# Zero products and the guard ahead of spreads, changed in the scans of the second layer

## The chip, the cores and the metric

The kernel runs as one program on one core of a Trainium2 chip. The metric is the device time of one execution in microseconds, and the figure compared is the median over runs. The engines are called TensorE (PE in the profile, PEld for its weight loads), VectorE (DVE), ScalarE (ACT), GpSimd (POOL) and SyncE (SP, which here only issues DMA transfers).

## The reference, cut to what matters

The network has four layers over 4 images of 64x64 positions and 96 channels. The first two layers are state space layers. Each expands to 192 inner channels, orders the 4096 positions of an image in four ways, and runs a recurrence with 16 states for each channel along each order:

```python
def step(h, inp):
    dt, u, Bl, Cl = inp
    h = h * jnp.exp(dt[..., None] * A) + (dt * u)[..., None] * Bl[:, :, None, :]
    y = jnp.einsum('bkdn,bkn->bkd', h, Cl)
    return (h, y)
```

For one image of one layer that is 4 orders x 192 channels x 16 states x 4096 steps. The two layers compute this in the same way and differ in the orders (diagonals and rings in the first layer; rows and columns, forwards and backwards, in the second), and in what is made of the sums afterwards. A feed-forward part of the second layer and the layers three and four follow; they have nothing to do with the change.

## The kernel before

**Tiling of a scan.** One *batch* is one image of one layer; there are eight, the first four of the first layer. A batch has 16 *segments* (four orders x four stretches of 1024 steps). A segment has 6 *channel blocks* of 32 channels, and a block has 4 *groups* of 4 states, so that a group is a tile of 128 partitions (32 channels x 4 states) by 1024 steps. A segment thus has 24 groups and a batch 384.

**What a group does** (lines of the kernel before):

- `spread_u` (L1098), once for a block: TensorE multiplies `dt*u` of 32 channels by a matrix of ones and zeros, which copies every channel to 4 partitions. Two products of 512 columns, each of them two rows in the profile, fill the PSUM tile `u`. There is one such tile, so the spread of the next block waits until the last group of this block has read it.
- `decay` (L1105): ScalarE computes `da`, the exponential of `dt*A`. Four buffers.
- `enter` (L1109): VectorE multiplies `u` by the B factors and writes `t`.
- `recur` (L1116): VectorE runs the recurrence over 1024 steps and writes `h`.
- `leave` (L1131): GpSimd multiplies `h` by the C factors and writes `hc`.
- `collect` (L1141): TensorE adds the 4 states of every channel into the PSUM tile `y`, four products of 256 columns side by side in the array (8 rows in the profile). `y` holds two blocks, so a pair of blocks is open at a time.

VectorE's order is fixed by hand: two enters, then two recurrences, and so on. Seen from the spread of a block: it becomes ready when the last enter of the block before has ended; VectorE then still has the last two recurrences of that block to do; after these it needs the new `u`.

After the last collect of a pair ScalarE copies `y` out (`copy_y`, L1177), TensorE transposes the copy (`turn`, L1189, 4 products) into the PSUM bank `m`, and ScalarE copies the result into rows (`keep_rows`, L1195).

**The next segment** is prepared beside this one (`prepare`). TensorE turns the inputs (`turn_x`, L923), multiplies them by the projections (L963) and adds four terms of the softplus in PSUM (`add`, L1047, 16 products for a segment, here called *sums of the softplus*). Each result goes through the same single bank `m`, and ScalarE must take it out (L937, L976, L978, L1050) before the next product can write there. ScalarE also does the pointwise steps (L1013 to L1021) and the logarithm (L1039).

**The order of the work** is computed while the program is built. `batch` hands all operations of a batch to a `Flow` with a cost, a due time and what each depends on. `Flow.run` takes the operation that can start first, by its own clock; among those that start within 0.1 us it takes the one that is due first. The spreads, decays, enters, recurrences and leaves are *hard*: while a hard operation of an engine is still to come, another operation of that engine is taken only if it is due earlier, or ends some time ahead of the hard one's due time. That time, the *guard*, is 4.2 us for TensorE and 0.5 us for the others. Each engine then executes its own list strictly in order, each instruction waiting for its semaphores.

Whenever an operation of TensorE is placed, `Flow` calls `keep_busy` (L1151) with the gap that the plan has ahead of it, less 2.0 us if the operation is hard (a spread) and less 0.1 us if not. `keep_busy` fills that gap with *zero products* (L1166): 32 columns of zeros times 256 columns, one for every 0.43 us. They leave the sums as they are. They are written into the open half of `y` (adding zero), or, when the last collected group was the last of its block, into the half that the next block will begin anew, or into the next `y` tile once the old one has been copied.

Between batches `side_by_side` runs the merging of one image and the projections and convolutions of another; the change does not touch it.

Of the kernel before, what the change touches and what calls it, by code (L numbers as in the profile page):

```python
# [38 lines left out]
NSG = NS // GS  # L39
# [3 lines left out]
class Kit:  # L43


    def __init__(self, tc, pool):
        self.tc, self.nc = tc, tc.nc
        nc = self.nc
        self.ident = self.t(pool, [128, 128], "ident")
        make_identity(nc, self.ident)  # L50
        self.eps = self.t(pool, [128, 1], "eps")
        nc.vector.memset(self.eps, 1e-5)
# [71 lines left out]
class Flow:  # L124

    def __init__(self, fill):
        self.fill, self.ops = fill, []

    def add(self, *args, **kw):
        op = Op(*args, **kw)
# [3 lines left out]
    def run(self):  # L136
        inside = set(map(id, self.ops))
        for op in self.ops:
            op.deps = [d for d in op.deps if id(d) in inside]
            op.left = len(op.deps)  # L140
            for d in op.deps:
                d.users.append(op)
        for op in reversed(self.ops):
            for d in op.deps:
                due = op.due - d.occ - (0.0 if d.engine == op.engine else d.lat)
                d.due = due if d.due is None else min(d.due, due)
        free, ready, hard = {}, {}, {}
        for op in self.ops:
            free.setdefault(op.engine, 0.0)
            ready.setdefault(op.engine, [])  # L150
            if op.hard:
                hard.setdefault(op.engine, []).append(op)
        for ops in hard.values():
            ops.sort(key=lambda op: -op.due)
        for op in self.ops:
            if not op.left:
                ready[op.engine].append(op)
        bank, drift, left, strict = 0.0, 0.0, len(self.ops), True
        while left:
            best = None  # L160
            for engine, ops in ready.items():
                if not ops:
                    continue
                first = hard.get(engine, [])
                while first and first[-1].left < 0:
                    first.pop()
                when = lambda op: max(free[engine], op.seen, op.after, bank if op.bank > 0 else 0.0)
                fits = ops
                if strict and first:
                    limit = first[-1].due + drift - (4.2 if engine == "PE" else 0.5)  # L170
                    fits = [
                        op
                        for op in ops
                        if op.hard or op.due <= first[-1].due or when(op) + op.occ <= max(limit, free[engine])
                    ]
                    if not fits:
                        continue
                soonest = min(map(when, fits))
                if soonest == math.inf:
                    continue  # L180
                op = min((op for op in fits if when(op) <= soonest + 0.1), key=lambda op: op.due)
                if best is None or when(op) < best[0]:
                    best = when(op), op
            if best is None:
                assert strict
                strict = False
                continue
            strict = True
            start, op = best
            engine = op.engine  # L190
            if engine == "PE":
                self.fill(free[engine], start - free[engine] - (2.0 if op.hard else 0.1))
            op.emit()
            left -= 1
            op.left = -1
            ready[engine].remove(op)
            done = op.fin = start + op.occ
            free[engine] = done
            if op.bank:
                bank = math.inf if op.bank > 0 else done + op.lat  # L200
            if engine == "DVE":
                drift = max(0.0, start - op.due)
            for user in op.users:
                near = user.engine == engine and not op.lands
                user.seen = max(user.seen, done if near else done + op.lat + op.slack)
                user.left -= 1
                if not user.left:
                    ready[user.engine].append(user)
        return drift
# [170 lines left out]
class Stream:  # L380
# [467 lines left out]
    def fetch(self, seg):  # L848
# [31 lines left out]
        if seg.bt.lay.ordered and seg.kd < 2:  # L880

            for j in range(SEG // 128):
                at = seg.i * SEG + j * 128
                seg.turned[j] = []
                for pos, n, token, step in diagonal_runs(seg.kd, at, at + 128):
                    ops.append(Op("SP", 0.1, partial(run, j, pos - at, n, token, step), lat=4.0))
                    seg.turned[j].append((pos - at, n, step < 0))
        elif seg.bt.lay.ordered:
            ops += [Op("POOL", 1.25, partial(gather, j), lat=4.0) for j in range(SEG // 128)]
        elif seg.kd % 2 == 0:  # L890
            ops.append(Op("SP", 0.1, whole, lat=5.0))
        else:
            ops += [Op("SP", 0.1, partial(columns, w), lat=5.0) for w in range(2)]
# [254 lines left out]
            )  # L1148
        self.open = None if gr.sg == NSG - 1 and cb % 2 else gr

    def keep_busy(self, now, gap):  # L1151


        lay = self.layers[0]
        if self.open:
            start = self.open.sg == NSG - 1
            half = 1 if start else self.open.cb % 2
            y = self.open.seg.y[:GC, half * 256 : (half + 1) * 256]
        elif self.vacant and now > self.vacant.fin + 0.5:
            if self.next_y is None:  # L1160
                self.next_y = self.k.t(self.ps_y, [128, CH], "y")
            y, start = self.next_y[:GC, :256], True
        else:
            return
        for _ in range(int(gap / 0.43)):
            self.nc.tensor.matmul(  # L1166
                y,
                self.zeros,
                lay.diag.rearrange("p h t c -> p (h t c)")[:, :256],
                start=start,  # L1170
                stop=start,
                tile_position=(0, 0),
            )
# [57 lines left out]
    def batch(self, segs):  # L1231


        slot, length = 6.74, 6.74 * NCB * NSG / 2
        flow, last = Flow(self.keep_busy), segs[-1]
        add = flow.add
        groups = {}
        dve = []
# [8 lines left out]
        for n, seg in enumerate(segs):  # L1247
            base, o, nxt = n * length, seg.o, seg.next
            prev = segs[n - 1] if n else None
            if nxt:  # L1250
# [5 lines left out]
                if far:  # L1256
                    far.fetched = self.fetch(far)
                    free = [nxt.o["X", j] for j in range(0, SEG // 128, 2)]
# [3 lines left out]
            for i in range(NG):  # L1262
# [6 lines left out]
                if sg == 0:  # L1269
                    if (n, cb) != (0, 0):  # L1270
# [14 lines left out]
                        hard=True,  # L1285
# [7 lines left out]
                    hard=True,  # L1293
# [8 lines left out]
                    hard=True,  # L1302
# [4 lines left out]
                for g2 in (groups[n, i - 1], gr):  # L1307
                    k0 = n * NG + g2.g
                    of = lambda name, back: groups[divmod(k0 - back, NG)].__dict__.get(name) if k0 >= back else None
                    start = base + i // 2 * slot + 2.24 + g2.g % 2 * 2.25  # L1310
# [7 lines left out]
                        hard=True,  # L1318
# [3 lines left out]
                    if not ends:  # L1322
# [8 lines left out]
                        hard=True,  # L1331
# [1107 lines left out]
```

## Time and profile before

| | us |
|---|---|
| median of 3 runs | 15246.63 (15242.52 to 15286.9) |
| profiled execution, its own time | 15391.0 |
| its span, first to last instruction | 15389.1 |
| VectorE busy in the span | 12831.6 (83%) |
| TensorE busy in the span | 13751.2 (89%) |
| VectorE idle ahead of `t` (enter), whole span | 281.2, of it 207.5 released by `u` on PE |
| mean granted TensorE clock | 0.88 of full speed |

The page gives, for each group of instructions, its line, engine, operation, operands and count, then the busy time, the mean duration of one in ns, and the idle time of its engine just before it with what ended that idle time. A product in 32-bit floats takes two rows of TensorE. Granted clock is the share of full speed at which TensorE ran; 0.50 in a stretch means half speed throughout.

### The profile page before, as it was taken

Reading aid. Unit: us, or ns where it says so; the run is one execution under the profiler, and the core shown is the slowest. Engines: PE = TensorE matmul, PEld = TensorE weight load, DVE = VectorE, ACT = ScalarE, POOL = GpSimd, SP = SyncE. Lnnn points to the kernel's source line nnn. Section 1 sums busy time; section 2 is a strip of 40 time slices with the busy share of each in tenths; the row PEclk is TensorE's granted clock in tenths of the full one; section 3 lists DMA queues with packets and bytes.
Section 4 is the critical chain, followed back from the end, with each engine's and each line's share of the span. In section 5 each row is a group of like instructions: output and inputs, shape, how many; then the busy total and the mean of one; then the engine's idle time right before and its main releaser. Section 6 shows DMA issues by size and latency. Waiting matters only on the chain. (4 is left out here: it accounts for less than half of the span.)

```text
span 15389.1 us, 225440 instructions
## 1 busy us (share of the span) xinstructions
PE 13751.2 (89%) x88567; PEld 5562.3 (36%) x88567; DVE 12831.6 (83%) x9645; ACT 8289.2 (54%) x13549; POOL 9204.4 (60%) x4657
## 2 busy tenths in 40 slices
PE   7999899989998999899989998999899889998877
PEld 3333333333333333333333333333333344443344
DVE  1999799969996999699979997999899856565655
ACT  3666466646664666466646665666566423232333
POOL 0898589858985888577747774777577620000123
PEclk9889888878898889888889898888899899998888
DMA  2333433343334333433343334333433400000122
GB/s 79 111 126 125 140 112 126 122 140 112 126 126 139 117 119 127 138 121 114 127 140 123 124 120 146 126 124 111 155 119 119 143 10 11 19 18 13 52 70 71
DMA packets 679264, 1639.33 MB, mean 107 GB/s; under 512 B 102822, under 2 KB 301227, under 8 KB 674428
## 3 DMA queue, kind: packets, MB, share of 16 engines
q1 hardware_dynamic: 641340, 1549.37, 31.7%
q0 software_dynamic: 36864, 75.55, 1.7%
q8 instruction: 700, 11.47, 0.3%
q14 instruction: 360, 2.95, 0.1%
HBM read 1295.03 MB, written 329.58 MB: 106 GB/s over the span
## 5 line engine op out<-in xcount | busy, mean ns | idle before, releaser
L1131 POOL TENSOR_TENSOR hc<-h,bc 128x1024 f32<-128x1024 f32 x3072 | 7203.9, 2363 | 2404.4 <-DVE h L1116 1934.0
L1116 DVE TENSOR_TENSOR_SCAN h<-da,state,t 128x1024 f32<-128x1024 f32 x2304 | 5276.6, 2333 | 30.6 <-ACT state L1127 18.5
L1105 ACT ACTIVATE da<-dts,L_A_logs 128x1024 f32<-128x1024 f32 x3072 | 3510.2, 1149 | 1237.7 <-DVE h L1116 1195.6
L1109 DVE TENSOR_TENSOR t<-u,bc 128x1024 f32<-128x1024 f32 x3072 | 3598.2, 1218 | 281.2 <-PE u L1098 207.5
L1166 PE MATMUL y<-L_diag,zeros 96*32 96x256 f32 x9734 | 2635.8, 410 | 0.0
L1141 PE MATMUL y<-hc,gather_y 128*32 128x256 f32 x24576 | 2434.5, 440 | 35.6 <-POOL hc L1131 34.8
L1098 PE MATMUL u<-dtu,spread 32*128 32x512 f32 x3072 | 1756.5, 696 | 523.9 <-DVE t L1109 517.2
L1116 DVE TENSOR_TENSOR_SCAN h<-da,t 128x1024 f32<-128x1024 f32 x768 | 1711.3, 2270 | 13.0 <-ACT da L1105 8.8
L1166 PEld LDWEIGHTS y<-L_diag,zeros 96*32 96x32 f32 x9734 | 1096.2, 118 | 1418.5 <-issue 664.3
L1141 PEld LDWEIGHTS y<-hc,gather_y 128*32 128x32 f32 x24576 | 723.1, 116 | 1692.2 <-issue 1227.2
L1098 PEld LDWEIGHTS u<-dtu,spread 32*128 32x128 f32 x3072 | 557.2, 201 | 1415.4 <-issue 933.1
L1692 DVE SCALAR_TENSOR_TENSOR hcv<-padv,taps,hcv 128x2048 f32<-128x2048 f32 x384 | 902.2, 2350 | 13.4
L1616 POOL MEMSET padp<- 128x2448 f32 x32 | 68.4, 2137 | 1392.9 <-PE d L1656 1374.8
L1656 PE MATMUL d<-padp,diag 32*32 32x512 f32 x25600 | 885.4, 600 | 2.0 <-ACT hcp L1671 2.0
L1050 ACT COPY dt<-m 96x512 f32<-96x512 f32 x512 | 297.1, 580 | 1056.3 <-PE m L1047 1056.1
L1047 PE MATMUL m<-dtu,ident 96*96 96x512 f32 x1024 | 591.3, 660 | 94.1 <-ACT xs L937 43.8
L963 PE MATMUL m<-area,proj 96*128 96x512 f32 (+1 forms) x1024 | 581.0, 689 | 43.2 <-ACT spare L1195 26.5
L1656 PEld LDWEIGHTS d<-padp,diag 32*32 32x32 f32 x25600 | 481.7, 103 | 372.2 <-issue 198.2
L963 PE MATMUL m<-xs,proj 96*128 96x512 f32 (+1 forms) x1024 | 558.0, 667 | 39.4 <-ACT spare L1195 26.0
L1047 PE MATMUL m<-dt,ident 96*96 96x512 f32 x1024 | 567.0, 637 | 0.0
L1047 PE MATMUL m<-sp_log,ident 96*96 96x512 f32 x1024 | 564.0, 634 | 0.0
L1047 PE MATMUL m<-sp_z,ident 96*96 96x512 f32 x1024 | 551.2, 621 | 0.0
(282 smaller groups left out, 15904.5 us busy)
## 6 DMA issues: line engine op xcount, KB each, us to landing
bc<-bc_dram SPq DMA_DIRECT2D x1024, 512.0 KB
dts<-dt_dram SPq DMA_DIRECT2D x768, 512.0 KB
dt_dram<-dt SPq DMA_DIRECT2D x256, 384.0 KB
y_tok<-spare SPq DMA_DIRECT2D x64, 768.0 KB
dt<-y_tok SPq DMA_DIRECT2D x128, 384.0 KB
x_tok<-area SPq DMA_DIRECT2D x32, 768.0 KB
z_t<-area SPq DMA_DIRECT2D x64, 384.0 KB
area<-x_tok SPq DMA_DIRECT2D x64, 384.0 KB
```

The lines of the kernel that those rows point to most:

```text
L963: nc.tensor.matmul(v.ps, seg.proj[:, src, to], seg.xs[:, src, chunks[j]], start=src == 0, stop=src == 1)
L1047: nc.tensor.matmul(v.ps, k.ident[:C, :C], term[:, half, chunks[j]], start=at == 0, stop=at == 3)
L1050: nc.scalar.copy(v.dt[:, half, chunks[j]], v.ps)
L1098: self.nc.tensor.matmul(seg.u[:, cols], self.spread[rows, :], seg.dtu[rows, half, cols], start=True, stop=True)
L1105: self.nc.scalar.activation(gr.da, gr.seg.dts[gr.cb], AF.Exp, scale=scale)
L1109: self.nc.vector.tensor_mul(gr.t, gr.seg.u, self.bc[:, 0, gr.sg, :])
L1116: self.nc.vector.tensor_tensor_scan(gr.h[:, order], gr.da[:, order], gr.t[:, order], start, op0=ALU.mult, op1=ALU.add)
L1131: self.nc.gpsimd.tensor_mul(gr.hc, gr.h, self.bc[:, 1, gr.sg, :])
L1141: nc.tensor.matmul(seg.y[at : at + GC, cb % 2 * 256 : (cb % 2 + 1) * 256], self.gather_y, gr.hc[:, part * 256 : (part + 1) * 256], start=g ...
L1166: self.nc.tensor.matmul(y, self.zeros, lay.diag.rearrange("p h t c -> p (h t c)")[:, :256], start=start, stop=start, tile_position=(0, 0),)
L1656: nc.tensor.matmul(pc[i][j * 32 : (j + 1) * 32, :], diag[mine, ON_PE.index(t), tap, :], pad[mine, j * 8 + dy : j * 8 + dy + 8, dx : dx + H ...
L1692: nc.vector.scalar_tensor_tensor(to, win, wt, to, op0=ALU.mult, op1=ALU.add)
```

## The change

In the batches of the second layer only:

- the guard of TensorE ahead of a spread's due time is 3.2 us in place of 4.2 us;
- zero products are placed only while a block's sums are open, that is after its first, second or third collect. None is placed between the last collect of a block and the first of the next, and none into a `y` tile that is not yet in use;
- the number of zero products in a planned gap is (gap - 0.15 us) x 1.4 / 0.43 us, also ahead of a spread, in place of (gap - 2.0 us or 0.1 us) / 0.43 us.

The batches of the first layer keep the guard, the places and the number. The flag `dense` is `lay.ordered`, which is true for the first layer alone.

```diff
-    def __init__(self, fill):
-        self.fill, self.ops = fill, []
+    def __init__(self, fill, guard):
+        self.fill, self.guard, self.ops = fill, guard, []
...
-                    limit = first[-1].due + drift - (4.2 if engine == "PE" else 0.5)
+                    limit = first[-1].due + drift - (self.guard if engine == "PE" else 0.5)
...
-                self.fill(free[engine], start - free[engine] - (2.0 if op.hard else 0.1))
+                self.fill(free[engine], start - free[engine], op.hard)
...
-    def keep_busy(self, now, gap):
+    def keep_busy(self, now, gap, hard, dense):
         lay = self.layers[0]
+        if dense:
+            count = int((gap - (2.0 if hard else 0.1)) / 0.43)
+        else:
+            count = int((gap - 0.15) * 1.4 / 0.43)
+            if self.open is None or self.open.sg == NSG - 1:
+                return
...
-        for _ in range(int(gap / 0.43)):
+        for _ in range(count):
...
-        flow, last = Flow(self.keep_busy), segs[-1]
+        dense = segs[0].bt.lay.ordered
+        flow, last = Flow(partial(self.keep_busy, dense=dense), 4.2 if dense else 3.2), segs[-1]
```

## The prediction, made before the changed kernel ran

> **What bounds the kernel now.** I read the page first: span, then the clock row, then the costliest groups.
>
> ```profile
> span 15389.1 us, 225440 instructions
> ...
> PEclk9889888878898889888889898888899899998888
> ...
> L1109 DVE TENSOR_TENSOR t<-u,bc 128x1024 f32<-128x1024 f32 x3072 | 3598.2, 1218 | 281.2 <-PE u L1098 207.5
> L1166 PE MATMUL y<-L_diag,zeros 96*32 96x256 f32 x9734 | 2635.8, 410 | 0.0
> L1098 PE MATMUL u<-dtu,spread 32*128 32x512 f32 x3072 | 1756.5, 696 | 523.9 <-DVE t L1109 517.2
> ```
>
> VectorE's enters and recurrences fill the scans, and what it loses there it loses ahead of `t`, waiting for a spread. Next the stage table, one row for each batch of the second layer (columns: length, busy time of PE, PEld, DVE, ACT, POOL, granted clock, DMA), and VectorE's group over these four batches:
>
> ```profile
> 6505.00:7830.90 1325.90, 1226.91 (x5830) 458.19 (x5828) 1289.75 (x768) 829.55 (x1225) 971.51 (x415) 0.88 0.36 116
> 7989.10:9311.50 1322.40, 1224.52 (x5830) 458.86 (x5828) 1289.80 (x768) 834.70 (x1230) 971.51 (x415) 0.88 0.36 116
> 9466.80:10781.00 1314.20, 1227.15 (x5830) 458.53 (x5828) 1290.01 (x768) 833.99 (x1230) 971.74 (x415) 0.88 0.36 117
> 10880.10:12185.40 1305.30, 1193.49 (x5854) 456.22 (x5852) 1289.26 (x768) 813.09 (x1203) 966.57 (x413) 0.90 0.36 116
> ```
>
> ```profile
> L1109 DVE TENSOR_TENSOR t<-u,bc 128x1024 f32<-128x1024 f32 x1536 | 1800.1, 1220 | 125.8 <-PE u L1098 125.4
> ```
>
> Lengths less VectorE's busy time: 36 + 33 + 24 + 16 = 109 us. So the change can win at most some 109 us (0.7%); it can lose more. One channel block takes 1289.7 / 96 = 13.43 us of VectorE's time.
>
> Then the timeline of TensorE, at a late spread and at two on time (columns: start, duration, instruction, count, idle before it and what ended it):
>
> ```profile
> 8033.69 1.46 PE L1166 MATMUL y<-L_diag,zeros 96*32 96x256 f32 x6
> 8040.03 1.13 PE L1189 MATMUL m<-ident,yc 128*128 128x128 f32 x4 [4.89 <-ACT xs L937]
> 8042.94 2.02 PE L1047 MATMUL m<-dtu,ident 96*96 96x512 f32 x2
> 8046.60 3.78 PE L1098 MATMUL u<-dtu,spread 32*128 32x512 f32 x4
> ...
> 8494.92 1.96 PE L963 MATMUL m<-area,proj 96*96 96x512 f32 x4 [0.21 <-ACT dt L976]
> 8496.83 1.96 PE L1098 MATMUL u<-dtu,spread 32*128 32x512 f32 x4
> 8508.50 2.75 PE L1166 MATMUL y<-L_diag,zeros 96*32 96x256 f32 x12
> ...
> 12164.28 0.66 PE L1189 MATMUL m<-ident,yc 128*128 128x128 f32 x4 [0.73 <-ACT yc L1177]
> 12167.53 2.11 PE L1098 MATMUL u<-dtu,spread 32*128 32x512 f32 x4 [2.59 <-DVE t L1109]
> ```
>
> A spread takes 1.96 us at full clock and 3.78 at half. VectorE needs it 4.4 us after it became ready (it has two recurrences to do until then). So it may start 2.4 us late at full clock, but only 0.6 at half. The first row group shows the loss: a turn waited 4.89 us for ScalarE to empty bank `m`, the idle time halved the clock, and VectorE stood for 5.5 us. Stretches of the clock's own length around it:
>
> ```profile
> 8035.61:8039.03 3.42, 0.00 (x0) 0.00 (x0) 3.42 (x3) 3.40 (x5) 2.74 (x2) 1.00 0.00 0
> 8039.03:8042.44 3.41, 2.40 (x14) 1.28 (x14) 3.41 (x3) 2.19 (x6) 1.92 (x1) 0.50 0.49 145
> 8052.68:8056.09 3.41, 3.41 (x12) 0.59 (x10) 3.41 (x3) 1.01 (x2) 1.22 (x1) 0.50 0.00 0
> 8056.09:8059.51 3.42, 3.42 (x5) 1.14 (x6) 3.42 (x4) 0.70 (x2) 2.35 (x1) 0.50 0.00 0
> ```
>
> The clock changes only on this grid of 3.41 us. Over all stretches of the second layer's scans, a full-speed stretch is followed by half speed when less than about 0.54 of it is work, counting a spread (32 rows of the array) at about a third. So a spread with 1 to 2 us of idle time ahead mostly drops the clock, and such a drop costs some 3.5 us of TensorE's time: 1.8 in the spread, the rest in what follows.
>
> Counting in the trace, spread by spread over the second layer (376, without the first two of each batch): 47 are late, by 107 us; 41 of these lie in spreads 2 to 5 of the four batches, 66 in all others.
>
> **The change part by part.**
>
> *What moves.* In the order of the built programs VectorE's own list of enters and recurrences is the same; TensorE, ScalarE (its evictions between the decays), GpSimd (the product of `dt` and `x` among the leaves) and SP (the loads `bc` and `dts` and the stores `dt_dram`, `bc_dram` among each other) are reordered in the second layer; the first layer's lists are identical. GpSimd has 971 busy us of 1322 and no VectorE wait is put down to it in these batches; the DMA loads release none of the idle time ahead of `t` or `h` either. I cost these two at 0; without that cover each would cost a 2.3 us step (the leave's mean).
>
> *Zero products.* Second layer: 2408 before, 2325 after. At (2.75 - 0.2)/6 = 0.43 us each the 83 are 36 us of TensorE's time in 5268, nothing on the path. What counts is where they lie: before, 664 stand between a block's last collect and the next spread; after, none.
>
> *Load of a block* at full clock: spread 1.96, collect 0.5 (16 rows take 1.07), sum of the softplus 0.95 (half of 1.91 at half clock), projection 0.98, turn or input turn 0.66, zero product 0.43. Before, the 376 blocks have 11.22 us on average, spread by only 0.5, and 4 exceed 12.4. After: 11.14 on average, spread by 1.13; 32 exceed 12.4 and 12 exceed 13.43, a block's whole time; but 59 lie under 10, where 7 did. The idle time ahead of a spread stays about 2 us on average.
>
> *First reading, by load.* Lateness for each spread in this trace (both layers, from spread 6 on): under 10 us 0; 10 to 11 0.155; 11 to 11.5 0.10; 11.5 to 12 0.29; over 12 0.41 to 0.44. On the new blocks (55, 117, 62, 94, 32): 0 + 18 + 6 + 28 + 13 = 65 us, against 66 now. Change: -1.
>
> *Second reading, by what stands last ahead of the spread:* zero products 0.17 us for each spread (287), sums 0.24 (207), projections 0.28 (96), a collect 0.003 (75), a turn 0 (15). After, 144 spreads follow a turn, 87 a sum, 63 a projection, 58 a collect, 8 an input turn, none a zero product: 0 + 21 + 17.5 + 0 + 0 = 38 us. Change: -28.
>
> *The turns.* The shorter guard moves 141 turns from behind a spread to straight ahead of one. There the spread queues behind last collect, ScalarE's copy (0.58 us) and the turn, and behind whatever `m` still holds. The trace has 15 such spreads, all on time, with 0.73 us of idle time in the row above, but most in light blocks. Bounds for the 144: 0, or as the worst class above, 144 x 0.28 = +40; the 4.89 us wait of the late example, if it came at each tenth, 14 x 5.5 = +77. I take 0 from the 15 rows, nearest in kind, with the first reading instead of the second, since that prices the load of these blocks.
>
> *Start of a batch.* Ahead of spread 4 the load goes from 11.2 to 13.5 us, ahead of spread 5 from 13.4 to 15.8 (12 sums in place of 10). In three of four batches both are late already, so each added us is lost: 3 x (2.3 + 2.4) = +14; bounds 0 and 4 x 4.7 x 2 at half clock = +38.
>
> *A rule against the change.* The Trainium skill, "TensorE: Matmul & The Clock Gate" (section "Why this matters for your kernels"), says to leave no idle gaps over about 3 us between bursts. The blocks without zero products at their end leave up to 3.7 us ahead of 43 spreads of 9.8 us load; by that rule these 43 drop the clock, an estimate of 43 x 3.5 = 150 us of TensorE's time, of which little is VectorE's as these are ready early. The trace is stricter on the drop (1 to 2 us beside a spread suffice, so the same happens before the change), and differs from the page's Part 1 on the return: there one busy window releases the clock, while above it stayed at 0.50 through fully busy stretches.
>
> Sum: -1 + 14 + 0 = +13 us. On the profiled execution 15391.0 + 13 = 15404; that stands 144 us over the median of the runs, so for the median 15247 + 13 = 15260.
>
> **The rivals.**
>
> *Slower: the turns gate the spreads.* Place: the turn ahead of two spreads in five. For it: the 4.89 us row; a turn cannot start before ScalarE, which stands in order behind decays that wait for VectorE (631 us of idle time ahead of L1105 in these batches). Against: the 15 on time. Price: 14 + 40 = +54 with the worst class, 14 + 40 + 77 = +131 with one long wait in ten: 15300 to 15378. It decides once a turn ends more than 2.4 us behind the spread's ready time, or 0.6 at half clock.
>
> *Faster: the spreads start earlier.* For it: 664 zero products (0.43 us each) leave the stretch ahead of spreads, and 30 us of the second layer's lateness lies behind such products; idle time is worth more to a late spread than clock. Price: -28 by the second reading, to -72 if only the start's 41 us remain less a few: 15175 to 15219.
>
> *It does little.* The clock drops as often, lateness shifts from block to block: -10 to +30. This is the sum's own case.
>
> **How the numbers follow.** 0.3% (46 us) is about what a measurement of this kernel can tell from no change. The sum's case, -30 to +60: 0.42 (faster 0.02, same 0.31, slower 0.09). Gating turns: 0.31 (slower 0.27, same 0.04). Earlier spreads: 0.27 (faster 0.23, same 0.04). Together faster 0.25, same 0.39, slower 0.36. The range reaches to the ends of both rivals, with a few us for a clock that drops more often: 15175 to 15390. The likeliest case's own range is 15217 to 15307.
>
> **What would show it.** VectorE's idle time ahead of L1109 in the second layer's batches, 125.4 now, at 110 to 170; the first layer's four batches as they were. Right on the turns: PE L1189 shows ScalarE waits of about 0.7 us (then the spread, on time). Wrong, slower: L1189 with waits of several us and spreads at half clock behind it, granted clock of these batches at 0.85 or less. Wrong, faster: idle time ahead of L1109 at 60 or less. It would be wrong altogether if the new order of GpSimd or SP put `h` or `dts` late: then VectorE would wait at L1116.

## The result and the profile after

The changed kernel takes 15362.14 us (median of 7 runs, 15317.96 to 15400.55); the kernel before, run beside it, takes 15261.04 us (7 runs, 15222.91 to 15286.9). The ratio is 1.0065, 95% interval 1.0048 to 1.0082: slower by 0.65%, or 101 us. That lies inside the predicted range and above the predicted 15260; it is where the slower rival stood, and above the likeliest case's own range (15217 to 15307).

From the page of the changed kernel: span, clock row, and the groups that answer to those shown before (zero products are L1172 now):

```profile
span 15398.8 us, 225149 instructions
...
PEclk9889888988888888888888888888888899998888
...
L1109 DVE TENSOR_TENSOR t<-u,bc 128x1024 f32<-128x1024 f32 x3072 | 3596.1, 1216 | 417.4 <-PE u L1098 344.8
L1172 PE MATMUL y<-L_diag,zeros 96*32 96x256 f32 x9568 | 2596.8, 414 | 0.0
L1098 PE MATMUL u<-dtu,spread 32*128 32x512 f32 x3072 | 1786.8, 707 | 387.5 <-DVE t L1109 379.8
```

The two spans differ by 10 us only, because the profiled execution of before stood 130 us over the median of its 7 runs and this one 38 us over its own. (The four stretches of other work behind the first-layer batches took 207 to 216 us each in the trace of before and 175 to 180 in this one; the change doesn't touch them.) So the batches have to be compared. The stage table of the changed kernel, one row for each batch of the second layer (length, busy time of PE, PEld, DVE, ACT, POOL, granted clock, DMA), and VectorE's group over these four:

```profile
6416.10:7755.50 1339.40, 1229.10 (x5782) 463.80 (x5782) 1291.99 (x768) 828.45 (x1225) 971.52 (x415) 0.87 0.36 115
7912.10:9257.40 1345.30, 1238.12 (x5782) 466.34 (x5781) 1292.37 (x768) 833.04 (x1230) 971.55 (x415) 0.86 0.36 114
9414.00:10759.20 1345.20, 1236.42 (x5782) 465.95 (x5782) 1292.33 (x768) 833.07 (x1230) 971.40 (x415) 0.86 0.36 114
10859.80:12208.80 1349.00, 1238.74 (x5832) 471.69 (x5832) 1292.15 (x768) 811.38 (x1203) 966.88 (x413) 0.86 0.35 112
```

```profile
L1109 DVE TENSOR_TENSOR t<-u,bc 128x1024 f32<-128x1024 f32 x1536 | 1800.2, 1218 | 227.9 <-PE u L1098 227.1
```

VectorE's busy time is nearly as before (1289.7 to 1292.2 us a batch on average). The four batches together grew from 5268 to 5379 us, by 111 us. VectorE's idle time ahead of `t` went from 125.8 to 227.9 us, by 102 us, which is nearly all of that; it is released by spreads, and ahead of L1116 VectorE waits 0.7 us in all four batches. TensorE has slightly less to do than before, and the clock went from 0.88 to 0.86.

What TensorE itself waited for in these batches tells where the loss begins. The waits of the kernel before (engine, tile and line, released by; us in total, times, longest):

```profile
PE u L1098 <- DVE t L1109: 231.1, 192, 2.9
PE m L963 <- ACT spare L1195: 37.8, 29, 1.6
...
PE m L1189 <- ACT xs L937: 15.5, 4, 4.9
```

and of the changed one (the turn is L1195 now, `copy_y` L1183):

```profile
PE m L1195 <- ACT dt L978: 103.2, 43, 2.4
PE u L1098 <- DVE t L1109: 88.7, 105, 2.1
PE m L1195 <- ACT dt L1050: 44.8, 36, 1.3
PE m L1195 <- ACT yc L1183: 38.6, 46, 2.4
PE m L1195 <- ACT xs L937: 32.0, 15, 3.2
```

Before, the largest wait of TensorE was harmless: a spread in its place early, waiting for VectorE to finish with `u` (231 us). That wait is the reserve of the spreads. After, 142 us of it are gone, and the turn waits for ScalarE instead: 22.2 us before, 238.5 after (its whole group). All waits of products that write bank `m` (L923, L963, L1047 and the turn) add up to 159 us before (39.4 + 50.1 + 47.3 + 22.2, from the groups of TensorE in the same stretch) and 332 after (34.3 + 25.4 + 34.2 + 238.5).

One place in the second of these batches shows the steps. First TensorE (start, duration, instruction, count, idle before it and what ended it):

```profile
8402.36 1.96 PE L963 MATMUL m<-area,proj 96*96 96x512 f32 x4
8404.25 0.64 PE L1141 MATMUL y<-hc,gather_y 128*32 128x256 f32 x8
8407.31 1.12 PE L1195 MATMUL m<-ident,yc 128*128 128x128 f32 x4 [2.42 <-ACT dt L978]
8408.35 3.77 PE L1098 MATMUL u<-dtu,spread 32*128 32x512 f32 x4
...
8413.92 3.73 PE L963 MATMUL m<-area,proj 96*96 96x512 f32 x4
8417.58 3.20 PE L1172 MATMUL y<-L_diag,zeros 96*32 96x256 f32 x7
...
8424.02 1.98 PE L1098 MATMUL u<-dtu,spread 32*128 32x512 f32 x4
...
8436.37 0.66 PE L1195 MATMUL m<-ident,yc 128*128 128x128 f32 x4 [1.28 <-ACT dt L1050]
8436.96 2.92 PE L1098 MATMUL u<-dtu,spread 32*128 32x512 f32 x4
...
8441.67 2.02 PE L1047 MATMUL m<-dtu,ident 96*96 96x512 f32 x2
...
8449.44 1.10 PE L1047 MATMUL m<-dtu,ident 96*96 96x512 f32 x2
...
8453.78 1.98 PE L1098 MATMUL u<-dtu,spread 32*128 32x512 f32 x4
```

ScalarE over the first wait:

```profile
8404.96 0.58 ACT L1183 COPY yc<-y 128x512 f32<-128x512 f32 x1 [0.95 <-PE y L1141]
8405.44 1.15 ACT L1105 ACTIVATE da<-dts,L_A_logs 128x1024 f32<-128x1024 f32 x1
8406.49 0.18 ACT L1127 COPY state<-h 128x1 f32<-128x1 f32 x1
8406.57 0.68 ACT L978 ACTIVATE dt<-m,L_dtb 96x512 f32<-96x512 f32 x1
```

and VectorE over the four spreads:

```profile
8412.16 2.36 DVE L1109 TENSOR_TENSOR t<-u,bc 128x1024 f32<-128x1024 f32 x2 [1.30 <-PE u L1098]
...
8426.04 2.36 DVE L1109 TENSOR_TENSOR t<-u,bc 128x1024 f32<-128x1024 f32 x2 [0.29 <-PE u L1098]
...
8439.91 2.36 DVE L1109 TENSOR_TENSOR t<-u,bc 128x1024 f32<-128x1024 f32 x2 [0.28 <-PE u L1098]
...
8455.80 2.36 DVE L1109 TENSOR_TENSOR t<-u,bc 128x1024 f32<-128x1024 f32 x2 [2.30 <-PE u L1098]
```

The projection leaves its result in `m` at 8404.3. ScalarE, in its own order, does the copy of `y`, a decay and a state first, and empties `m` at 8407.25. Only then can the turn start, and the spread queues behind it. The clock falls to half at 8407.2, so the spread takes 3.77 us, the projection behind it 3.73 (1.96 at full clock) and seven zero products 3.20 (1.70 in the block before). The clock is back by 8420.8, but a second turn waits 1.28 us ahead of the third spread, and from 8437.9 to 8448.1 the clock is at half again: the sums there take up to 2.02 us, 1.10 at full clock. The following spreads start late in turn, and the fourth, behind the block of eight sums, costs VectorE 2.30 us. This pattern comes 35 times in the second layer; the block of eight sums alone costs 50.6 us over them.

Counted spread by spread over the second layer (376): before, 47 are late, by 107 us in all; after, 138, by 209. Spreads at half clock (longer than 2.6 us) went from 69 to 110 and cost about the same (50 and 44 us). Spreads at full clock that started more than 2.6 us after their ready time went from 32 to 100; the lateness of full-clock spreads went from 58 to 165 us. The loss in these two traces is there: the mean start moved from 0.99 to 1.73 us after ready, and 2.4 is where a full-clock spread begins to cost.

### The profile page after: what moved, and what is told of

It reads as the page before. It is cut to its first block, busy times and chain, and to the rows that moved or that the text cites. A ratio compares the mean times of both kernels' runs of the same rounds, so it can differ in the third digit from the quotient of the medians.

```text
span 15398.8 us, 225149 instructions
## 1 busy us (share of the span) xinstructions
PE 13710.2 (89%) x88401; PEld 5589.3 (36%) x88401; DVE 12849.3 (83%) x9645; ACT 8284.6 (54%) x13549; POOL 9207.0 (60%) x4657
## 5 line engine op out<-in xcount | busy, mean ns | idle before, releaser
L1116 DVE TENSOR_TENSOR_SCAN h<-da,state,t 128x1024 f32<-128x1024 f32 x2304 | 5272.9, 2329 | 34.5 <-ACT state L1127 21.7
L1172 PE MATMUL y<-L_diag,zeros 96*32 96x256 f32 x9568 | 2596.8, 414 | 0.0
L1116 DVE TENSOR_TENSOR_SCAN h<-da,t 128x1024 f32<-128x1024 f32 x768 | 1710.8, 2269 | 13.2 <-ACT da L1105 9.5
L1172 PEld LDWEIGHTS y<-L_diag,zeros 96*32 96x32 f32 x9568 | 1078.3, 119 | 1393.9 <-issue 646.1
L1047 PE MATMUL m<-dtu,ident 96*96 96x512 f32 x1024 | 612.0, 682 | 83.5 <-ACT dt L1050 27.6
L963 PE MATMUL m<-xs,proj 96*128 96x512 f32 (+1 forms) x1024 | 594.9, 705 | 22.7 <-ACT spare L1201 8.6
L1056 POOL TENSOR_TENSOR dtu<-dt,xs 96x1024 f32<-96x1024 f32 x128 | 301.6, 2357 | 515.8 <-ACT dt L1050 465.3
L963 PE MATMUL m<-area,proj 96*128 96x512 f32 (+1 forms) x1024 | 587.3, 696 | 24.9 <-ACT dt L978 12.3
L1047 PE MATMUL m<-sp_z,ident 96*96 96x512 f32 x1024 | 585.7, 656 | 0.0
L1047 PE MATMUL m<-dt,ident 96*96 96x512 f32 x1024 | 584.7, 655 | 0.0
```

Source lines behind the costliest of these rows:

```text
L963: nc.tensor.matmul(v.ps, seg.proj[:, src, to], seg.xs[:, src, chunks[j]], start=src == 0, stop=src == 1)
L1047: nc.tensor.matmul(v.ps, k.ident[:C, :C], term[:, half, chunks[j]], start=at == 0, stop=at == 3)
L1116: self.nc.vector.tensor_tensor_scan(gr.h[:, order], gr.da[:, order], gr.t[:, order], start, op0=ALU.mult, op1=ALU.add)
L1172: self.nc.tensor.matmul(y, self.zeros, lay.diag.rearrange("p h t c -> p (h t c)")[:, :256], start=start, stop=start, tile_position=(0, 0),)
```

## The experiments

All ratios are to the kernel before on the same chip, with their 95% intervals; they are not exactly the quotients of the medians. "Idle ahead of t" is VectorE's, in the second layer's four batches of the profiled execution, "bank m" the sum of the idle time ahead of the products that write it, and "reserve" the spreads' wait for VectorE, in the same stretches, each from one trace; zero products are those of the second layer.

| run | guard | zero products | bank m | reserve | idle ahead of t | ratio |
|---|---|---|---|---|---|---|
| before | 4.2 | 2408 | 159 | 231 | 125.8 | |
| c0_before_again | 4.2 | 2408 | 153 | 235 | 80.6 | 0.9999 [0.9974, 1.0025] |
| e8_guard42_factor1 | 4.2 | 1643 | 208 | 355 | 105.9 | 1.0005 [0.999, 1.0019] |
| e1_fill_alone | 4.2 | 2307 | 148 | 306 | 122.9 | 1.0028 [1.0014, 1.0041] |
| e2_guard_alone | 3.2 | 2180 | 329 | 127 | 155.3 | 1.0037 [1.0016, 1.0057] |
| e3_factor_one | 3.2 | 1523 | 382 | 171 | 148.5 | 1.0033 [1.0019, 1.0047] |
| e10_factor12 | 3.2 | 1886 | 356 | 150 | 128.9 | 1.0022 [1.0008, 1.0036] |
| e11_trim_three_four | 3.2 | 2146 | 338 | 130 | 145.6 | 1.0025 [1.001, 1.0041] |
| e12_trim_five_zero | 3.2 | 2181 | 343 | 95 | 159.5 | 1.0056 [1.0031, 1.0081] |
| after | 3.2 | 2325 | 332 | 89 | 227.9 | 1.0065 [1.0048, 1.0082] |
| c1_after_again | 3.2 | 2325 | 331 | 99 | 202.0 | 1.0052 [1.0033, 1.0072] |
| e9_no_singles | 3.2 | 2216 | 333 | 79 | 192.9 | 1.0073 [1.005, 1.0096] |
| e5_turns_guarded | 3.2 | 2187 | 332 | 146 | 245.7 | 1.0101 [1.0078, 1.0124] |
| e6_no_zeros | 3.2 | 0 | 460 | 335 | 267.6 | 1.0122 [1.0085, 1.0158] |

### Each part alone

The first two runs undo one part of the change each. e1 keeps the new zero products and the old guard:

```diff
-        flow, last = Flow(partial(self.keep_busy, dense=dense), 4.2 if dense else 3.2), segs[-1]
+        flow, last = Flow(partial(self.keep_busy, dense=dense), 4.2 if dense else 4.2), segs[-1]
```

> The changed kernel with the guard of the second layer put back to 4.2 us, so that only the placing and the number of the zero products differ from the kernel before; turns stand behind the spreads again (3 of 376 spreads follow a turn, 144 in the changed kernel). If the loss comes from the order that the shorter guard makes (a turn that waits for ScalarE straight ahead of a spread, half clock after it): VectorE's idle time ahead of L1109 in the second layer's batches at 110 to 150 us, near the 126 of before, and 15240 to 15290 us, at most 30 over the kernel before. If it comes from the zero products (none between the last collect and the spread, 1.4 times as many between collects): 200 us or more there and about 15360 us.

Measured: 15417.71 us against 15370.92, ratio 1.0028 [1.0014, 1.0041]. Waits of TensorE and VectorE's group in e1:

```profile
PE u L1098 <- DVE t L1109: 305.7, 209, 4.2
PE m L963 <- ACT spare L1201: 53.4, 38, 2.6
```

```profile
L1109 DVE TENSOR_TENSOR t<-u,bc 128x1024 f32<-128x1024 f32 x1536 | 1798.5, 1218 | 122.9 <-PE u L1098 122.8
```

The idle time is what the first case said, the time is not: 0.28% is some 43 us, over the 30 allowed. The turn waits 16.6 us in all, the reserve is larger than before the change, and no zero product stands directly ahead of a spread any more. Where the 0.28% lies, this one profile does not show: its idle time (122.9 us) stands between the two traces of the kernel before (125.8 and 80.6). What grew against both are blocks made fuller by the factor: 51 blocks of projections with 4 zero products in place of 3, from the seventh spread of a batch on, are late by 22.7 us in e1, 3.1 in before and 4.1 in c0. The fullest 23 (13.2 us of work on average, some 15 zero products in place of 10 or 11) are late by 24.9 us, but by 19.0 in before and 9.3 in c0.

e2 keeps the new guard with the zero products as they were:

```diff
-        if dense:
-            count = int((gap - (2.0 if hard else 0.1)) / 0.43)
-        else:
-            count = int((gap - 0.15) * 1.4 / 0.43)
-            if self.open is None or self.open.sg == NSG - 1:
-                return
+        count = int((gap - (2.0 if hard else 0.1)) / 0.43)
```

> The changed kernel with the zero products placed and counted in the second layer as before, so that only the guard of 3.2 us is new; 144 of 376 spreads follow a turn. If the order is the cause: idle time ahead of L1109 in the second layer at 190 to 240 us, about 15340 to 15370 us. If the zero products are the cause: 110 to 150 us, about 15260 us.

Measured: 15442.66 us, ratio 1.0037 [1.0016, 1.0057]. Waits and VectorE's group in e2 (the turn is L1190 here):

```profile
PE u L1098 <- DVE t L1109: 126.5, 95, 3.3
PE m L1190 <- ACT dt L978: 103.2, 43, 2.4
PE m L1190 <- ACT dt L1050: 43.9, 35, 1.3
```

```profile
L1109 DVE TENSOR_TENSOR t<-u,bc 128x1024 f32<-128x1024 f32 x1536 | 1799.0, 1217 | 155.3 <-PE u L1098 154.9
```

The largest wait of the turn is here to the tenth of a microsecond, and all its waits come to 236.2 us, without any new zero product. So they come from the guard. The idle time lies between the two cases that were expected (190 to 240, or 110 to 150 us), so neither part is the whole cause. The costs of the two parts, 0.28% and 0.37%, add up to the 0.65% of both together; with intervals of 0.13 to 0.2 points either way, and 0.52% in the repeat c1, so exact a sum is luck. The places differ, too: in e2 the block of eight sums costs 6.4 us, while 43 blocks behind a turn that waits 2.4 us, which end in six zero products directly ahead of the spread, cost 42.9 us (18.6 in the changed kernel, where these six are gone and the block has nine others in place of seven).

### How many zero products

e3 is the changed kernel with the factor 1.0, e10 with 1.2, in place of 1.4; e8 is e3 with the guard of 4.2. In each the order of all other work is that of its guard.

```diff
-            count = int((gap - 0.15) * 1.4 / 0.43)
+            count = int((gap - 0.15) * 1.0 / 0.43)
```

> The changed kernel with the factor 1.4 replaced by 1.0: 1510 zero products in place of 2305 in the second layer, the same order of all else. If too many zero products delay the spreads (load of a block 11.14 us falls to 10.25): idle time ahead of L1109 falls from 228 us to under 150. If the clock is the cause (idle time drops it, and the block after runs at half speed): fewer zero products lower the clock further, below 0.85 in these batches, and the idle time stays at 200 to 280 us, 15350 to 15420 us.

> The changed kernel with the factor 1.2 in place of 1.4: 1870 zero products in the second layer, between the 1510 of factor 1.0 (idle time ahead of L1109 149 us) and the 2305 of factor 1.4 (228 us). If load is the cause: 150 to 190 us, between the two, by the blocks of 12 us or more (40, 48, 87). If the loss at 1.4 was the chance of one alignment with the clock's grid: anything from 120 to 240 us, in no order.

> Guard 4.2 us, zero products only while a block's sums are open, factor 1.0: the order of before, and no block of the second layer over 12.4 us but the four at the start of a batch (load 10.39 us on average, before 11.22). If late spreads come from blocks whose own work, zero products included, nearly fills the 13.43 us: idle time ahead of L1109 in the second layer falls to 60 to 100 us, 25 to 65 us faster than before. If fewer zero products cost more through the clock than they free: 130 us or more there, clock of these batches under 0.86.

Measured: e3 1.0033 [1.0019, 1.0047], e10 1.0022 [1.0008, 1.0036], e8 1.0005 [0.999, 1.0019], with 148.5, 128.9 and 105.9 us of idle time. At the guard of 3.2 the factor 1.4 costs 0.3 to 0.4% over 1.2, at 4.2 some 0.2% over 1.0; these compare runs on different chips, and the intervals of c1 and e10, and of e1 and e8, still touch. The idle times are not in the order of the factors: 148.5, 128.9, and 227.9 or 202.0 us for 1.0, 1.2 and 1.4, where load alone was to put e10 between the other two. e8 lies between its two cases as well. Neither direction is free: with 1.0 the clock of these batches is 0.83 to 0.84 in e3 and 0.85 to 0.87 in e8, and e3 is no better than e10. None of the three is faster than the kernel before; e8, nearest to it, can't be told from it.

e6 takes all zero products out of the second layer, with the guard of 3.2:

```diff
-            if self.open is None or self.open.sg == NSG - 1:
-                return
+            return
```

> The changed kernel without any zero product in the second layer's scans; the same order of all else (the sums are unchanged, as only zeros were added). It prices the zero products as a whole. If they earn their place by the clock: granted clock of these batches at 0.70 or less, idle time ahead of L1109 at 300 us or more, over 15430 us. If real work alone (8.57 us of 13.43 at full clock) has room enough even at half clock: under 200 us and 15330 us or less, and then the zero products themselves are part of the loss.

Measured: 15571.14 us, ratio 1.0122 [1.0085, 1.0158]. The granted clock of the four batches is 0.71 to 0.72; 212 of the 376 spreads are at half clock and these cost 184 us of the idle time (267.6, short of the 300 expected); 140.8 us of the lateness lie behind turns (31.3 in the changed kernel). So the zero products do earn their place: e3 and e10, with the same order and fewer of them than the changed kernel, stand at 1.0033 and 1.0022.

### Which blocks

In the changed kernel the block of eight sums has 12.0 us of work, a single zero product among it. e9 takes out every zero product that would stand alone:

```diff
-            if self.open is None or self.open.sg == NSG - 1:
+            if self.open is None or self.open.sg == NSG - 1 or count < 2:
```

> The changed kernel, with no zero product where the count for a gap comes to one. This takes 109 zero products out of the second layer, and most of all the one in the block of eight sums that follows a turn (load 12.0 to 11.6 us); all else stands as in the changed kernel. If the load of the heavy blocks is the cause: the 51 us of lateness behind that block fall to 5 to 25 us, idle time ahead of L1109 from 228 to 170 to 205 us. If the clock that drops at the turn is the cause, 0.43 us cannot matter: 215 to 240 us.

Measured: 1.0073 [1.005, 1.0096]; the block of eight sums, at 11.6 us now, still costs 43.7 us (50.6 with the single one, 42.8 in the repeat c1). The idle time, 192.9 us, is what the theory of load said, but not from this block, where it said 5 to 25. In e10 the very same block costs 5.0 us, and in e3 10.6. Its own work is not the reason; what stands ahead of it is. Ahead of it stand two blocks with 9 and 7 zero products (7 and 6 in e10), and ahead of these the turn that waits 2.42 us.

e11 and e12 split this. e11 uses the factor 1.2 only where the open sums are those of channel blocks 3 and 4 (the block with the waiting turn and the one behind it: in each of the 35 patterns three zero products less), e12 only for channel blocks 5 and 0 (the two blocks with the sums: two less). The edit of e11:

```diff
-            count = int((gap - 0.15) * 1.4 / 0.43)
+            trim = self.open is not None and self.open.cb in (3, 4)
+            count = int((gap - 0.15) * (1.2 if trim else 1.4) / 0.43)
```

> The changed kernel, but in layer 2 the factor is 1.2 in place of 1.4 where the open sums are those of channel blocks 3 and 4; the order of all other work is the same. It takes one zero product out of the block 'P2 f4 c P2 c T' and two out of the block behind it, 'P2 f4 c f5 c' (f = zero product, P = projection, m = sum, X = transpose, T = turn, c = collect; a number says how many stand in a row). Theory 'cold zeros': the turn that stands straight ahead of a spread waits for ScalarE (2.4 us of idle PE), the clock falls to half at this spread, and the zero products behind it cost 0.86 us each in place of 0.43; these three are what pushes the following sums out. Then the last collect of the second block ends some 0.7 us after the gates are ready in place of 2.2, the block of eight sums two blocks on (its own work unchanged) costs VectorE 5 to 15 us in all in place of 51, and the idle time ahead of t in the four layer-2 batches falls from 228 to 130 to 160 us; ratio to the kernel before 1.000 to 1.004. Rival 'sums' blocks too full': that block and the one ahead of it are as full as in the changed kernel, so it keeps 40 to 51 us, and the idle time stays at 200 to 228 us; ratio 1.005 to 1.008.

> The other half: factor 1.2 where the open sums are those of channel blocks 5 and 0, so that the two blocks with the sums themselves have one zero product less each (f7 becomes f6, the single one ahead of the last two pairs goes). Theory 'cold zeros': the block ahead of them is late as before (last collect 2.2 us after the gates), the two products give back some 0.9 us of about 3.7, so the block of eight sums keeps 25 to 40 us and the idle time ahead of t in layer 2 is 180 to 215 us; ratio 1.004 to 1.007. Rival 'sums' blocks too full': 5 to 10 us there, 130 to 160 us in all, ratio 1.000 to 1.004.

Measured for e11: 1.0025 [1.001, 1.0041], idle time 145.6 us. The last collect ahead of the second spread ends 0.02 us after ready on average (2.19 in the changed kernel, 1.08 in c1), and the block of eight sums, unchanged, costs 12.7 us. Here the theory of cold zero products met its figures for the block, the idle time and the ratio; the collect ended earlier than the 0.7 us that it said. For e12: 1.0056 [1.0031, 1.0081], 159.5 us. The ratio is what that theory said, and the block ahead is as late as before (2.28 us), but the block of eight sums costs 6.5 us, where the theory said 25 to 40 and the rival 5 to 10, and the idle time is the rival's, too. So neither is right alone. What both runs fit is that lateness is handed on from block to block: two or three zero products less in the first two of these four blocks, or in the last two, bring the last spread from 3.69 us after ready (3.59 in c1) to 2.22 (e11) or 1.66 (e12), below the 2.4 us from which it costs. Whether one place is worth more than the other is open, since the two intervals overlap.

### The turn, or whatever stands there

e5 leaves the guard at 3.2 and tells the planner that a turn takes 1.5 us in the second layer, so that turns stay behind the spreads (35 spreads follow a turn in place of 144):

```diff
-        dense = segs[0].bt.lay.ordered
+        dense = self.dense = segs[0].bt.lay.ordered
...
-        t = flow.add("PE", 0.5, partial(self.turn, seg, pair), [copied, *self.rows_free(seg, pair)], lat=0.25, due=at + 15.0, bank=1)
+        t = flow.add("PE", 0.5 if self.dense else 1.5, partial(self.turn, seg, pair), [copied, *self.rows_free(seg, pair)], lat=0.25, due=at + 15.0, bank=1)
```

> The changed kernel, but the planner is told in layer 2 that a turn takes 1.5 us of the TensorE in place of 0.5, so that with the guard of 3.2 us turns no longer go in straight ahead of a spread: 35 spreads follow a turn in place of 144, while the fullest blocks are fuller than in the changed kernel (55 above 12.4 us of work in place of 32). Theory 'cold zeros': without the waiting turn the spread of channel block 5 keeps its clock (about 2.3 us long in place of 3.56) and the idle time ahead of t in layer 2 falls to 120 to 170 us in spite of the fuller blocks; ratio 1.001 to 1.004. Rival 'how full a block is decides': 55 blocks above 12.4 us make it 200 us or more, ratio 1.005 or more.

Measured: 15411.2 us against 15265.51, ratio 1.0101 [1.0078, 1.0124], idle time 245.7 us. The theory said 120 to 170 and is refuted in this form; the rival, that fullness decides, said 200 or more and a ratio of 1.005 or more, which came. Waits of TensorE in e5, and a late place in it:

```profile
PE u L1098 <- DVE t L1109: 146.2, 136, 3.2
PE m L963 <- ACT dt L978: 85.9, 38, 2.4
PE m L1047 <- ACT dt L1050: 67.1, 53, 2.2
```

```profile
8457.34 0.64 PE L1141 MATMUL y<-hc,gather_y 128*32 128x256 f32 x8
8460.39 2.02 PE L963 MATMUL m<-xs,proj 96*96 96x512 f32 x2 [2.42 <-ACT dt L978]
8462.35 3.78 PE L1098 MATMUL u<-dtu,spread 32*128 32x512 f32 x4
```

The turn has only 51.8 us of idle time ahead of it, but the same 2.42 us now stand ahead of a projection, and all waits on bank `m` come to 332 us as in the changed kernel. So the wait does not belong to the turn: the guard of 3.2 lets a product of bank `m` in between the last collect and the spread, here a projection, and it waits until ScalarE has emptied the bank. e5's blocks are also fuller, and its trace has both: of 225.8 us of lateness 85.6 lie behind the 55 blocks above 12.4 us of work (70.5 behind 32 in the changed kernel), and 43.8 behind 35 blocks that end in one projection as above, with spreads of 3.35 us on average. So e5 doesn't separate the wait from the fullness. Every kernel with the guard of 3.2 waits longer on bank `m` (329 to 460 us) than every one with 4.2 (148 to 208), and where there are zero products its reserve is smaller (79 to 171 us against 231 to 355); e6, without them, has 335. That the waits eat the reserve is therefore likely, but no run takes them away and leaves the rest: a second bank for the product ahead of a spread was not tried. Nor does the reserve alone give the loss: e9 has the smallest, and less idle time than the changed kernel.

### Controls

c0 is the kernel before once more, c1 the changed one.

> The kernel before once more, as if it were a changed one: ratio 1.000, and a second profile of it. It shows how far the batches of the first layer, whose instructions no experiment changes, differ between executions (so far 5271 to 5341 us for the four), and whether the idle time ahead of L1109 in the second layer repeats at 126 us within 15.

> The changed kernel once more, on the chip of the experiments. If the loss belongs to the program: 200 to 240 us of idle time ahead of t in layer 2 again, ratio 1.0045 to 1.0085. If the profile of the changed kernel was an unlucky lie of the clock's steps: 130 to 190 us, with the ratio nearer to 1.003.

Measured: c0 0.9999 [0.9974, 1.0025] with 80.6 us of idle time; c1 1.0052 [1.0033, 1.0072] with 202.0 us. Of the 376 spreads 33 are late in c0, by 61.5 us, and 116 in c1, by 182.9. The loss belongs to the program. A single profile's idle time is good to some 25 to 45 us: 125.8 and 80.6 for the one kernel, 227.9 and 202.0 for the other.

## Why the prediction was right and wrong

**The number: inside the range by its width.** The sum said +13 us, 15260, and +101 was measured. The range reached to the ends of both rivals; the case that the sum stood for, with 0.42, ended at 15307, and what came was nearest to the rival with 0.31. That 15362 lies inside is the rival's merit and not the sum's.

**What bounds the kernel: right.** The loss (102 us of idle time between the profiles, 121 between their repeats, 101 us in the medians) is VectorE waiting for spreads. The forecast for that idle time, 110 to 170 us, was missed (227.9), and the sign named for a slower kernel came in part: spreads at half clock behind turns, but turns that wait 3.2 us at most, and a clock of 0.86 to 0.87, not 0.85 or less. GpSimd and SyncE, costed at nothing, stayed hidden: VectorE doesn't wait at L1116, and collects wait 20 us for GpSimd's products after 11.

**The limit of 2.4 us: right,** and it is what decides: 165 of 209 us of lateness come from full-clock spreads.

**The turns, taken at 0: the step that failed.** The 15 turn-ended spreads of the trace were all on time, and each turn there waited no more than 0.73 us. After the change the 191 turns of the second layer wait 238.5 us, 1.25 us on average, and 2.4 in the 43 cases that wait for the emptying behind a projection. The prediction had this wait in its slower rival (a turn cannot start before ScalarE, which stands behind decays), and that rival's price, +54 to +131, held the measured +101. Its place was right and its form was not quite: the turn-ended spreads themselves lose 31 us over 144, close to the +40 of the worst class, and none waits 4.89 us. The rest appears behind other blocks, those that end in sums above all; e11 and e12 fit that it is handed on to them, and how much of it is stays open.

**First reading, -1: wrong.** By its rates the new blocks were to lose 65 us; they lost 173. Blocks under 10 us of work, priced at 0, lost 18.6; those of 11.5 to 12 lost 76.8 in place of 28. A load counts TensorE's work in a block and not the waits in it, and the rates were measured where bank `m` waited 159 us, not 332. It also prices each block by itself, while e9 and e10 show the same block of eight sums at 43.7 and 5.0 us, by what stands before it. (By the costs of this reading 16 of the new blocks exceed 13.43 us, not 12.)

**Second reading, -28: wrong by its class of sums.** Priced at 0.24 us each, the 87 spreads behind sums lost 1.15 each (100.4 us). Projections were about right (22.8 for 17.5), and collects lost 18.6 where 0 was said.

**Zero products, 36 us "nothing on the path": right in number** (2408 to 2325) and wrong in sense. Those that moved into the blocks do cost once the reserve is small: with the guard of 3.2, e10's 439 fewer leave 128.9 us of idle time where the changed kernel has 227.9 and 202.0. For the faster rival, the tail of a block did become free of zero products, and with the guard of 4.2 the reserve rose from 231 to 306 us (e1), but the same factor filled other blocks, and the kernel was 0.28% slower.

**Start of a batch, +14: open.** Spreads 2 to 5 of the four batches lost 40.8 us before and 35.7 after; in the repeats 27.9 (c0) and 47.9 (c1).

**The clock: not as the sum's case said.** There it was to drop as often as before. It fell from 0.88 to 0.86, and the spreads at half clock rose from 69 to 110, but those cost 44 us after 50. What the lower clock adds is rather in the work behind them, as in the seven zero products of 3.20 us above. The rule weighed against the change (the Trainium skill, "TensorE: Matmul & The Clock Gate", section "Why this matters for your kernels": no idle gaps over about 3 us) pointed the same way, but the gap ahead of the drop above was 2.42 us.

## What to carry to other kernels

An engine that waits for the bottleneck is holding a reserve: before moving work ahead of an operation that gates the bottleneck, find how large that wait is (231 us here) and what the moved work itself waits for, not only how long it runs. A product that shares one PSUM bank can bring the wait for its emptying with it (22.2 us for the turns where they stood behind spreads, 238.5 ahead of them), and the planner's time for the product itself (0.5 us for the turn) doesn't show it. A price taken from a trace for "so much work in a block" holds only as long as the waits in the block, and the blocks before it, stay as they are.

## What was not expected of the hardware

- The clock's fall costs less than its figure suggests: without zero products it is 0.72 in place of 0.88 to 0.89 in these batches, a fifth less, and the four batches grow from 5219 us (c0) or 5268 (before) to 5415, by 3 to 4% (with the guard of 3.2 besides).
- One program's idle time differs between executions by tens of us: 80.6 and 125.8 us in the second layer of the kernel before, and 83 to 158 us in the first layer, whose instructions are the same in all of these runs.
- The turn's wait for ScalarE behind a projection is almost the same in every kernel with the new order: 103.2 or 103.3 us in e2, e3, e9 to e12, c1 and the changed kernel, with granted clocks from 0.83 to 0.88 (116.9 in e6, at 0.72). It seems to follow from ScalarE's order, copy of `y`, decay and state ahead of the emptying (0.58, 1.15, 0.18 and 0.68 us above), rather than from TensorE's clock; no run changes that order.
